# One sequence kernel's tables: the "into the states" table built from parameter rows in DRAM, and the scale moved to the "out of the states" table

## The chip, the cores and the metric

The kernel runs on one core of a Trainium2 chip. Its time is the device time of one execution in microseconds (us); the median of three runs before the change is 983.03 us (983.0 to 983.55). The core has a matrix engine (PE, whose weight loads are listed apart as PEld), a vector engine (DVE), an activation engine (ACT), a general engine (POOL) and SP, which here only issues DMA transfers. ACT and POOL issue transfers too. Each engine takes its instructions strictly in the order in which they were compiled, and an instruction whose input is late holds up all that stand behind it.

## The reference, cut to what matters

`x` is 64 batches by 64 heads by 1024 places. Each head is convolved causally with its own kernel of 1024 taps, a sum of 64 damped oscillations, after masking by a length per batch. What comes out goes through a mixture of 64 low-rank experts, 16 per token, and is added to `x`:

```python
dtA = A * dt[:, None]                       # A = -exp(log_A_real) + 1j * A_imag
P = dtA[:, :, None] * jnp.arange(length)
Cs = Cc * (jnp.exp(dtA) - 1.0) / A
K = 2.0 * jnp.einsum('hn,hnl->hl', Cs, jnp.exp(P)).real
...
y = irfft(rfft(u_m, n) * rfft(K, n))[..., :Lq] + u_m * D[:, None]   # then masked again
...
scores = xf @ Wr.T                          # xf = y, token by token
gates = softmax(top_k(scores, 16))
h = einsum('nd,krd->nkr', xf, A);  out = 2 * einsum('nkr,kdr->nd', h * G, B)
```

Everything is in float32.

## The kernel before, in words

The 64 heads are worked in 8 groups of 8; a group is 4 pairs of heads, and a pair fills 128 partitions (2 heads x 64 oscillations). The 1024 places are 8 blocks of 128. A convolution (`conv(g, ...)`) takes each pair through three parts. `into_states` multiplies the blocks of `x` by the table `bt` (products `pu`, place on the partitions) and ACT copies the result from PSUM to `s`; `recur` carries the states from block to block on DVE with the three columns `turn`; `inside` multiplies `x` with the Toeplitz matrix `toep` of a head's first 128 taps, and `across` adds to the same PSUM tile (`pc`) what comes out of the states by the table `w`. DVE masks the result into `y`.

`tables(g)` makes these tables. With the oscillation on the partitions and the place 0 to 128 along the free dimension it forms exp(place x dt_re) on ACT (`mag`), the turns place x tu (`f`, in two parts tu_hi and tu_lo), rounds and clamps them on DVE, and takes sine and cosine on ACT. The products of magnitude and circle are `w`. ACT and DVE then scale `w` by the pair's coefficients (`alpha`, `nbeta`, `nalpha`) into `b`; PE transposes `b` (tile `pb`, line 326), so that the place stands on the partitions, and ACT copies it to `bt` (lines 328 and 330). From `b` PE also sums the taps over the oscillations (`pk`, line 293); ACT copies them to `ks`, DVE adds D, and SP writes them to DRAM (`krows`, line 303) and reads them back as the Toeplitz matrix (line 305). In the first group all this is cut finer, since nothing else is there to run.

After a group's convolution, `gates(g, y)` finds its 16 experts per token (products `psh`, transposes `psc`, then a chain of DVE instructions), `spread_gates` spreads the gates over partitions through DRAM (`gx`, loads from POOL's queue), and `first(g, y, ...)` makes the first expert product: 14 products of 16 matmul records each (`h`, line 553), in four PSUM banks (`ps_f`). DVE and POOL add and gate these and POOL stores them. When all 8 groups are done, `second` makes the other expert product from what was stored.

**The order of the work.** The functions are generators: `conv` yields at places where the main loop issues one or more products of the group before, and it calls `step(n)` to issue n pieces of `tables(g + 2)`, the tables of the group after. This gives each instruction its rank. A planner then puts the instructions of each engine in order by simulated time: the first in rank of those that are ready. So ready work of a low rank can come early, where an engine would idle. Some instructions are pinned: `issue_after(i)` puts what a block holds for the engine of `i` behind `i`, on that engine alone; `keep_in_program_order` pins one instruction behind the one before it.

**Buffers.** `bt`, `toep`, `mag`, `f`, `k`, `sn` and `ks` have one buffer each; `w` and `turn` have two. The PSUM pool `ps_k` has two banks, shared by `pu`, `pb`, `pk`, `psh`, `psc` and `pg`. The loads of `x` (four buffers of a pair each) are issued by SP, and wait until `inside` of the pair that had the buffer is done.

Of the kernel before, what the change touches and what calls it, by code (L numbers as in the profile page):

```python
# [37 lines left out]
F32 = mybir.dt.float32  # L38
I32 = mybir.dt.int32
AF = mybir.ActivationFunctionType  # L40
# [4 lines left out]
P = 128  # L45
# [9 lines left out]
HG = 8  # L55
# [37 lines left out]
def body(ctx: ExitStack, tc, x, xo, lens, par, dvec, at, bm, wt, cst, out):  # L93
# [140 lines left out]
    tabs = {}  # L234
    scales = {}

    def tables(g):

        j0 = g * GP
        wide = [P, GP, NW]

        def new(t, name=None):
            return tabp.tile(wide, F32, tag=t, name=f"{name or t}_{g}")

        mag, f, k = new("mag"), new("f"), new("k")
        for i in range(GP):
            nc.scalar.activation(mag[:, i, :], lv, AF.Exp, scale=dt_re[:, j0 + i : j0 + i + 1])
        tt(f, tu_hi[:, j0 : j0 + GP].unsqueeze(2).to_broadcast(wide),  # L250
           lv.unsqueeze(1).to_broadcast(wide), ALU.mult)
        yield
        ts(k, f, MAGIC, ALU.add, MAGIC, ALU.subtract)
        yield
        tt(f, f, k, ALU.subtract)
        yield
        for i in range(GP):
            stt(f[:, i, :], lv, tu_lo[:, j0 + i : j0 + i + 1], ALU.mult, f[:, i, :], ALU.add)
            if i % 2:
                yield  # L260
        ts(f, f, HALF_IN, ALU.min, -HALF_IN, ALU.max)

        sh, sn = new("k", "sh"), new("sn")
        nc.scalar.activation(sh, f, AF.Sin, scale=math.pi)
        nc.scalar.activation(sn, f, AF.Sin, scale=2.0 * math.pi)
        nc.scalar.activation(sh, sh, AF.Square)
        nc.scalar.activation(sh, sh, AF.Copy, scale=-2.0, bias=1.0)
        yield
        w = tab2.tile([P, 2, GP, NW], F32, tag="w", name=f"w_{g}")
        tt(w[:, 1], mag, sn, ALU.mult)  # L270
        yield
        tt(w[:, 0], mag, sh, ALU.mult)
        yield
        alpha, nbeta, nalpha = (scales[q] for q in ("alpha", "nbeta", "nalpha"))
        bt = tp.tile([P, GP, 2 * P], F32, tag="bt", name=f"bt_{g}")

        def others():
            return (tab2.tile([P, 3, GP], F32, tag="turn", name=f"turn_{g}"),
                    tp.tile([P, HG, P], F32, tag="toep", name=f"toep_{g}"))

        if g == 0:
            turn, toep = others()
            tabs[g] = (w, bt, turn, toep)
        h0 = g * HG
        all_rows = tabp.tile([2, GP, P], F32, tag="ks", name=f"ks_{g}")

        def kernels(bbs, i):


            n = i + 2 * len(bbs)  # L290
            pk = ps_k.tile([2, n - i, P], F32, tag="pk", name=f"pk_{g}_{i}")
            for m, bb in enumerate(bbs):
                nc.tensor.matmul(pk[:, 2 * m : 2 * m + 2, :], lhsT=heads, rhs=bb[:, :, 0, :],  # L293
                                 start=True, stop=True)
            ks = all_rows[:, i:n, :]
            nc.scalar.copy(ks, pk)
            return ks, i, n

        def rows(ks, i, n):

            tt(ks[:, :, 0], ks[:, :, 0], d_sb[:, j0 + i : j0 + n], ALU.add)
            row = krows[h0 + 2 * i : h0 + 2 * i + 1, :]
            nc.sync.dma_start(
                krows[h0 + 2 * i : h0 + 2 * n, P - 1 :].rearrange("(i a) l -> a i l", a=2), ks)
            nc.sync.dma_start(toep[:, 2 * i : 2 * n, :],
                              bass.AP(row.tensor, row.offset, [[1, P], [KROW, 2 * (n - i)], [1, P]]))

        bbs, halves = [], []
        for i in range(GP):
            j = j0 + i  # L310
            re, im = w[:, 0, i, :P], w[:, 1, i, :P]
            if i % 2 == 0:
                bb = tabp.tile([P, 2, 2, P], F32, tag=("sn", "k")[i // 2], name=f"b_{g}_{i}")
                bbs.append(bb)
            b = bb[:, i % 2]
            for c, by in enumerate((alpha, nbeta)):
                if g == 0:
                    ts(b[:, c, :], re, by[:, j : j + 1], ALU.mult)
                else:
                    nc.scalar.activation(b[:, c, :], re, AF.Copy, scale=by[:, j : j + 1])  # L320
            stt(b[:, 0, :], im, nbeta[:, j : j + 1], ALU.mult, b[:, 0, :], ALU.add)
            stt(b[:, 1, :], im, nalpha[:, j : j + 1], ALU.mult, b[:, 1, :], ALU.add)
            if g == 0 or i % 2 == 0:
                pb = ps_k.tile([P, 1 if g == 0 else 2, 2 * P], F32, tag="pk", name=f"pb_{g}_{i}")
            for c in range(2):
                nc.tensor.transpose(pb[:, i % 2 if g else 0, (1 - c) * P : (2 - c) * P], b[:, c, :], ident)  # L326
            if g == 0:
                nc.scalar.copy(bt[:, i, :], pb[:, 0])
            elif i % 2:
                nc.scalar.copy(bt[:, i - 1 : i + 1, :], pb)  # L330
            if g == 0 and i % 2:
                halves.append(kernels(bbs[i // 2 :], i - 1))
            if g == 0 and i == 3:
                rows(*halves[0])
            yield
        if g:
            turn, toep = others()
        V.tensor_copy(turn[:, 0:2], w[:, :, :, P])
        ts(turn[:, 2], turn[:, 1], -1.0, ALU.mult)
        if g == 0:  # L340
            yield
            rows(*halves[1])
            return
        ks = kernels(bbs, 0)
        yield
        rows(*ks)
        tabs[g] = (w, bt, turn, toep)


    def new(name, w=NP, dtype=F32, keep=False):  # L350
# [117 lines left out]
    wa, wb = [], []  # L468
    marks = {}
    sums = factors_by_identity(*wa_quarters, wa)  # L470
    steps0 = tables(0)
    next(steps0)
    for _ in some(sums, 1):
        pass
# [3 lines left out]
    e_re = new("ere")  # L478
    n_re, n_im, t2 = new("nre"), new("nim"), new("t2")
    alpha, nbeta, nalpha = (new(n, keep=True) for n in ("alpha", "nbeta", "nalpha"))  # L480
    beta = new("beta")

    def products():
        ts(e_re, s2, -1.0, ALU.mult, 1.0, ALU.add)
# [27 lines left out]
        ts(nalpha, alpha, -1.0, ALU.mult)  # L512

    together(products(), some(steps0, 2))
    scales.update(alpha=alpha, nbeta=nbeta, nalpha=nalpha)

    for _ in some(sums, 7):
        pass
# [5 lines left out]

    def masks():
        lens_f = prep.tile([P, NB], F32, tag="lensf", name="lens_f")
        V.tensor_copy(lens_f, lens_sb)
        tt(mask, feat.unsqueeze(2).to_broadcast([P, NBLK, NB]),
           lens_f.unsqueeze(1).to_broadcast([P, NBLK, NB]), ALU.is_lt)
# [13 lines left out]
    def seven(fac, rf, j, name, finish, second_early=False):  # L543

        def product(n, bank=None, more=False):
            first = bank is None
            if first:
                bank = ps_f.tile([P, 2, HT], F32, tag="pf", name=f"{name}_{j}_{n}")  # L550
            for ii in range(2):
                for k in range(KH):
                    nc.tensor.matmul(  # L553
                        bank[:, ii, :],
                        lhsT=fac[n - 1][:, k, (j + ii) * P : (j + ii + 1) * P],
                        rhs=rf[n - 1][:, k, :],
                        start=(first and ii == 0 and k == 0),
                        stop=(ii == 1 and k == KH - 1 and not more),
                        skip_group_check=True,
                    )  # L560
            return bank

        def new(t, n=0):
            return fp.tile([P, 2, HT], F32, tag=t, name=f"{name}_{j}_{t}{n}")

        c11 = product(1, more=True)
        p1 = new("p", 1)
        nc.scalar.copy(p1, c11)
        yield
        if second_early:  # L570
            product(2, c11)
            yield
        p6 = product(6)
        u2 = new("u2")
        tt(u2, p1, p6, ALU.subtract)
        yield
        if not second_early:
            product(2, c11)
            yield
        p7 = product(7)  # L580
        u3 = new("u3")
        tt(u3, p7, u2, ALU.add)
        yield
        c12 = product(5, more=True)
        c22 = new("p", 5)
        stt(c22, u3, -1.0, ALU.mult, c12, ALU.subtract)
        yield
        p4 = product(4)
        yield
        product(3, c12)  # L590
        finish(j, c11, u2, u3, c12, p4, c22)
        yield


    def conv(g, steps, out):
# [89 lines left out]
        if g == 0:  # L685
            into_states(2)
            into_states(3)
            first_two = inside(0), inside(1)
            across(*first_two[0], True)
            across(*first_two[1])  # L690
            recur(2, 3)
            last_two = inside(2), inside(3)
            yield
            across(*last_two[0], True)
            across(*last_two[1])
            return
        yield
        step(4)
# [5 lines left out]
        recur(2, 3)  # L704
        out_of(1)
        yield
        step(5)
        yield
        out_of(2)
        yield  # L710
# [553 lines left out]
```

## Time and profile before

The profiled execution took 983.15 us; its span, from the first to the last instruction, is 981.3 us. The granted PE clock is full throughout.

| what | us |
|---|---|
| PE busy | 967.1 |
| DVE busy | 717.5 |
| ACT busy | 159.7 |
| POOL busy | 332.3 |
| start of the first `psh` of groups 0 to 7 | 51.0, 123.6, 185.3, 262.0, 338.7, 415.3, 492.0, 567.8 |

The time from one `psh` to the next is what one group takes: 76.7 us in groups 3 to 6. After 568 us only expert products follow, and the change doesn't reach them. Matmuls are pipelined: each record includes some waiting inside the engine, so the records of PE overlap, and the chain (which takes the time from one piece to the next) tells what an instruction adds. "Idle before" is an engine's idle time ahead of an instruction, with the one that ended it.

### The profile page before, as it was taken

To read this page: it belongs to the slowest core of one execution; us is meant where nothing else is said; L and a number is where in the kernel's file an instruction comes from. 1 tells how busy PE (TensorE), PEld (TensorE's weight loads), DVE (VectorE), ACT (ScalarE), POOL (GpSimd) and SP (SyncE) were. 2 spreads that over 40 slices of the span, in tenths; PEclk is the share of its full clock that TensorE was granted. 3 is DMA by queue.
4 is the path that set the end of the run, shared out by engine and by line. 5 is a ranking of instruction groups with operands and counts; after the bars stand their busy time and mean duration, and the time that the engine had idled before them with its cause. 6 is when DMAs were issued, how large, how long until landed. Compare 5 with 4: busy or idle time off the path is not lost.

```text
span 981.3 us, 11964 instructions
## 1 busy us (share of the span) xinstructions
PE 967.1 (99%) x4312; PEld 722.8 (74%) x4312; DVE 717.5 (73%) x1681; ACT 159.7 (16%) x310; POOL 332.3 (34%) x285
## 2 busy tenths in 40 slices
PE   7999999999999999999999999999999999999998
PEld 2476656676676686586676678888888888888887
DVE  8889698587487597587566669788866785686674
ACT  5245051420231231131001000000000000000000
POOL 0212121032023022122123112246645663754565
PEclk9999999999999999999999999999999999999999
DMA  7915243325315315415405254573674466268432
GB/s 279 235 50 162 73 150 105 108 81 161 108 70 145 126 41 156 140 55 156 135 27 166 76 177 161 200 290 110 214 258 130 169 207 232 88 215 269 128 117 98
DMA packets 67457, 143.99 MB, mean 147 GB/s; under 512 B 9479, under 2 KB 18247, under 8 KB 67399
## 3 DMA queue, kind: packets, MB, share of 16 engines
q1 hardware_dynamic: 49378, 94.40, 28.8%
q0 software_dynamic: 16864, 47.22, 15.5%
q10 hardware_dynamic: 1156, 1.61, 0.6%
q8 instruction: 34, 0.56, 0.2%
q14 instruction: 25, 0.20, 0.1%
HBM read 94.89 MB, written 47.25 MB: 145 GB/s over the span
## 4 chain that ended last, share of the span: by engine, by line
PE 94%; DVE 4%; DMA 0%; issue 0%; POOL 0%; ACT 0%; DVEq 0%
PE h L553 39%; PE s L1033 34%; PE pc L644 6%; PE pu L618 5%; PE pc L653 5%; PE psh L721 3%; PE pb L326 1%; PE pk L293 1%; DVE hg L355 1%; PE pg L765 0%; PE psc L730 0%; DMA par_sb<-in_par 0%; DVE y L661 0%; DVE ty L355 0%; DVE f L366 0%
## 5 line engine op out<-in xcount | busy, mean ns | idle before, releaser
L366 DVE SCALAR_TENSOR_TENSOR s<-s,turn 128x128 f32<-128x128 f32 (+1 forms) x558 | 142.9, 303 | 34.0 <-ACT s L623 28.0
L553 PE MATMUL h<-y,waa 128*128 128x256 f32 x512 | 121.8, 384 | 0.0
L553 PE MATMUL h<-ty,was 128*128 128x256 f32 x512 | 116.9, 381 | 0.0
L553 PE MATMUL h<-y,was 128*128 128x256 f32 x512 | 116.6, 381 | 0.0
L553 PEld LDWEIGHTS h<-y,waa 128*128 128x128 f32 x512 | 93.9, 190 | 28.7 <-issue 16.8
L553 PEld LDWEIGHTS h<-ty,was 128*128 128x128 f32 x512 | 96.5, 190 | 18.1 <-issue 5.4
L553 PEld LDWEIGHTS h<-y,was 128*128 128x128 f32 x512 | 96.5, 190 | 17.9 <-issue 5.2
L803 POOL TENSOR_TENSOR hg<-h_p,gx 128x512 f32<-128x512 f32 x16 | 27.0, 1689 | 218.6 <-DVE h_p L366 215.0
L803 POOL TENSOR_TENSOR hg<-h_u,gx 128x512 f32<-128x512 f32 x32 | 47.1, 1474 | 123.0 <-DVE h_u L355 122.2
L661 DVE TENSOR_TENSOR y<-pc,mask 128x512 f32<-128x512 f32 x64 | 42.3, 684 | 35.4 <-PE pc L653 35.4
L1047 ACT COPY p<-s 128x512 f32<-128x512 f32 x28 | 16.4, 586 | 312.9 <-PE s L1033 301.5
L900 POOL TENSOR_TENSOR o<-o,acc_a 128x512 f32<-128x512 f32 x32 | 48.0, 1519 | 42.7 <-DMA r<-hg_dram 10.8
L644 PE MATMUL pc<-x,toep 128*128 128x512 f32 x128 | 61.5, 605 | 0.0
L553 PE MATMUL h<-ty,waa 128*128 128x256 f32 x256 | 58.7, 381 | 0.0
L355 DVE TENSOR_TENSOR hg<-hg 128x512 f32<-128x512 f32 x64 | 42.8, 689 | 19.0 <-POOL hg L803 18.0
L776 POOL DMA_DIRECT2D gx<-gt_dram x56 | 33.5, 630 | 66.2 <-DMA gt_dram<-gt 66.2
L553 PEld LDWEIGHTS h<-ty,waa 128*128 128x128 f32 x256 | 47.9, 190 | 10.2 <-issue 3.9
L618 PE MATMUL pu<-x,bt 128*64 128x448 f32 x256 | 55.1, 553 | 0.0
L653 PE MATMUL pc<-s,w 64*128 64x448 f32 x248 | 54.7, 561 | 0.0
L355 DVE TENSOR_TENSOR o<-o,s 128x512 f32<-128x512 f32 (+1 forms) x53 | 35.6, 672 | 25.3 <-PE s L1033 18.8
L900 POOL TENSOR_TENSOR o<-o,b_room 128x512 f32<-128x512 f32 x32 | 49.9, 1581 | 9.8 <-DVE b_room L355 9.8
L623 ACT COPY s<-pu 128x448 f32<-128x448 f32 x62 | 33.0, 532 | 119.7 <-PE pu L618 119.6
(231 smaller groups left out, 1586.5 us busy)
## 6 DMA issues: line engine op xcount, KB each, us to landing
x<-in_x SPq DMA_DIRECT2D x32, 512.0 KB
hg_dram<-hg POOLq DMA_DIRECT2D x16, 1024.0 KB, 5.5
o<-in_xo SPq DMA_DIRECT2D x64, 256.0 KB
out<-o SPq DMA_DIRECT2D x63, 256.0 KB
gx<-gt_dram POOLq DMA_DIRECT2D x56, 256.0 KB, 6.3
qy<-hg_dram SPq DMA_DIRECT2D x28, 512.0 KB
r<-hg_dram SPq DMA_DIRECT2D x26, 512.0 KB
hg_dram<-hg POOLq DMA_DIRECT2D x16, 768.0 KB, 4.3
```

The source lines that it names most:

```text
L355: V.tensor_tensor(out=o, in0=a, in1=b, op=o_)
L366: V.scalar_tensor_tensor(out=o, in0=a, scalar=s, in1=b, op0=o1, op1=o2)
L553: nc.tensor.matmul(bank[:, ii, :], lhsT=fac[n - 1][:, k, (j + ii) * P : (j + ii + 1) * P], rhs=rf[n - 1][:, k, :], start=(first and ii == ...
L618: nc.tensor.matmul(pu[hh * NS : (hh + 1) * NS, :], lhsT=bt[:, i, (1 - c) * P + hh * NS : (1 - c) * P + (hh + 1) * NS], rhs=xt[:, hh, : NCH ...
L623: marks["s"] = nc.scalar.copy(s[:, c], pu.rearrange("p (k b) -> p k b", b=NB))
L644: nc.tensor.matmul(pc, lhsT=toep[:, 2 * i + hh, :], rhs=xt[:, hh, :], start=True, stop=False)
L653: m = nc.tensor.matmul(pcs[hh][:, NB:], lhsT=w[o : o + NS, c, i, 1:], rhs=s[o : o + NS, c].rearrange("p k b -> p (k b)"), start=False, sto ...
L661: marks["y"] = V.tensor_tensor(out=y[:, :, i // 2, 2 * (i % 2) + hh, :], in0=pcs[hh].rearrange("p (k b) -> p k b", b=NB), in1=mask, op=ALU ...
L776: i = queue.dma_start(gx[:, ii, :], gt_dram[g, c * n : (c + 1) * n, :].unsqueeze(1).to_broadcast([n, RANK, TOK]),)
L803: G.tensor_tensor(out=o, in0=a, in1=b, op=op)
L900: tc.keep_in_program_order(G.tensor_tensor(out=o, in0=a, in1=b, op=op_))
L1033: nc.tensor.matmul(bank[:, ii, :], lhsT=left_[i - 1][:, k, ii * P : (ii + 1) * P], rhs=right_[i - 1][:, k, :], start=(first and ii == 0 an ...
```

## The change

For the first group nothing changes but the names of buffers; `masks`, which runs on DVE during its convolution, also turns the sign of `nbeta` back into `beta`, which the later groups need. From the second group on, the table into the states is no longer scaled, transposed and copied. It is formed a second time, with the place already on the partitions, and without the coefficients; these go into the table out of the states instead (`o`, which takes the place of `w`), and the taps of the kernel are summed from `o`.

To form it, the parameters `dt_re`, `tu_hi` and `tu_lo` are needed as rows. Once, at the end of group 0's convolution, `parameter_rows` transposes the three on PE into one `ps_k` tile, copies it on ACT and writes it to DRAM (`trows`). Each group then loads its part of each row, repeated over all partitions, into the buffers of `mag`, `f` and the new one-buffer tile `turned`, and goes through exponential, rounding and circle again, with the scalar `place` (the partition's number) as factor. Two DVE products make `bt`. The pieces that `tables` yields are fewer (11 instead of 13), and the step in the middle of `conv` issues 6 instead of 5.

```diff
+    def circle(sh, sn, f, sign=1.0):
+        nc.scalar.activation(sh, f, AF.Sin, scale=math.pi)
+        nc.scalar.activation(sn, f, AF.Sin, scale=sign * 2.0 * math.pi)
+        nc.scalar.activation(sh, sh, AF.Square)
+        nc.scalar.activation(sh, sh, AF.Copy, scale=-2.0, bias=1.0)
...
+    def kernels(g, ks, re, i, n):
+        pk = ps_k.tile([2, n - i, P], F32, tag="pk", name=f"pk_{g}_{i}")
+        for m in range(0, n - i, 2):
+            nc.tensor.matmul(pk[:, m : m + 2, :], lhsT=heads, rhs=re[:, i + m : i + m + 2, :],
+                             start=True, stop=True)
+        nc.scalar.copy(ks[:, i:n, :], pk)
+
+    def rows(g, ks, i, n):
+        j, h = g * GP + i, g * HG + 2 * i
+        tt(ks[:, i:n, 0], ks[:, i:n, 0], d_sb[:, j : j + n - i], ALU.add)
+        nc.sync.dma_start(
+            krows[h : h + 2 * (n - i), P - 1 :].rearrange("(i a) l -> a i l", a=2), ks[:, i:n, :])
+
+    def toeplitz(g, toep, i, n):
+        row = krows[g * HG + 2 * i : g * HG + 2 * i + 1, :]
+        nc.sync.dma_start(toep[:, 2 * i : 2 * n, :],
+                          bass.AP(row.tensor, row.offset, [[1, P], [KROW, 2 * (n - i)], [1, P]]))
+
+    def tables(g):
...
+        mag, f, both_ = new("mag"), new("f"), turned(g)
+        k, sn = both_[:, 0], both_[:, 1]
+        for i in range(GP):
+            nc.scalar.activation(mag[:, i, :], lv, AF.Exp, scale=dt_re[:, j0 + i : j0 + i + 1])
...
+        ts(f, f, HALF_IN, ALU.min, -HALF_IN, ALU.max)
+        circle(k, sn, f)
+        yield
+        tt(sn, mag, sn, ALU.mult)
+        tt(k, mag, k, ALU.mult)
+        turn, toep = others(g)
+        V.tensor_copy(turn[:, 0:2], both_[:, :, :, P])
+        ts(turn[:, 2], turn[:, 1], -1.0, ALU.mult)
+
+        def row(t, n):
+            nc.sync.dma_start(flat(t), trows[n, j0 : j0 + GP, :].rearrange("j q -> (j q)").partition_broadcast(P))
+
+        mag, f = new("mag", "rmag"), new("f", "rf")
+        row(mag, 0)
+        row(f, 1)
+        yield
+        alpha, beta, nbeta = (scales[q] for q in ("alpha", "beta", "nbeta"))
+        o = tab2.tile([P, 2, GP, NW], F32, tag="w", name=f"w_{g}")
+        for i in range(GP):
+            j = j0 + i
+            for c, by in enumerate((alpha, beta)):
+                nc.scalar.activation(o[:, c, i, :], k[:, i, :], AF.Copy, scale=by[:, j : j + 1])
+            for c, by in enumerate((nbeta, alpha)):
+                stt(o[:, c, i, :], sn[:, i, :], by[:, j : j + 1], ALU.mult, o[:, c, i, :], ALU.add)
+            if i == 1:
+                yield
+        ks = rows_tile(g)
+        kernels(g, ks, o[:, 0, :, :P], 0, GP)
+        yield
+        both_ = turned(f"{g}r")
+        lo, place = both_[:, 1], feat[:, 0:1]
+        row(lo, 2)
+        mag, f, lo, k = flat(mag), flat(f), flat(lo), flat(both_[:, 0])
+        nc.scalar.activation(mag, mag, AF.Exp, scale=place)
+        ts(f, f, place, ALU.mult)
+        rows(g, ks, 0, GP)
+        yield
+        ts(k, f, MAGIC, ALU.add, MAGIC, ALU.subtract)
+        tt(f, f, k, ALU.subtract)
+        yield
+        stt(f, lo, place, ALU.mult, f, ALU.add)
+        ts(f, f, HALF_IN, ALU.min, -HALF_IN, ALU.max)
+        circle(k, lo, f, -1.0)
+        yield
+        bt = tp.tile([P, GP, 2 * P], F32, tag="bt", name=f"bt_{g}")
+        for c, t in enumerate((lo, k)):
+            tt(bt[:, :, c * P : (c + 1) * P], mag.rearrange("p (i q) -> p i q", q=P),
+               t.rearrange("p (i q) -> p i q", q=P), ALU.mult)
+        yield
+        toeplitz(g, toep, 0, GP)
+        tabs[g] = (o, bt, turn, toep)
...
     def masks():
         lens_f = prep.tile([P, NB], F32, tag="lensf", name="lens_f")
+        ts(beta, nbeta, -1.0, ALU.mult)
...
+    def parameter_rows():
+        pr = ps_k.tile([NP, 3, P], F32, tag="pk", name="par_rows")
+        for n, v in enumerate((dt_re, tu_hi, tu_lo)):
+            nc.tensor.transpose(pr[:, n, :], v, ident)
+        r = tabp.tile([NP, GP, P], F32, tag="ks", name="par_rows_sb")[:, :3, :]
+        nc.scalar.copy(r, pr)
+        nc.scalar.dma_start(trows.rearrange("k j q -> j k q"), r)
...
             across(*last_two[0], True)
             across(*last_two[1])
+            with tc.issue_after(marks["s"].ins):
+                parameter_rows()
             return
...
-        step(5)
+        step(6)
```

`marks["s"]` is, at that place, the last ACT copy of `s` in the first group's convolution.

## The prediction

> **What bounds the kernel now.** I read the busy shares first, then the chain that ended last.
>
> ```profile
> span 981.3 us, 11964 instructions
> PE 967.1 (99%) x4312; PEld 722.8 (74%) x4312; DVE 717.5 (73%) x1681; ACT 159.7 (16%) x310; POOL 332.3 (34%) x285
> ...
> PE 94%; DVE 4%; DMA 0%; issue 0%; POOL 0%; ACT 0%; DVEq 0%
> ```
>
> The matmul engine is the bound almost everywhere, so time is gained by taking work off PE, and lost where PE is made to wait. The chain in order of time prices what the change removes; this is its stretch around the end of one group's convolution:
>
> ```profile
> 322.37 0.22 PE pb L326 x2
> 322.59 3.46 PE h L553 x16
> ...
> 336.54 0.81 PE pb L326 x6
> 337.34 0.43 PE h L553 x2
> 337.78 0.96 PE pk L293 x4
> 338.73 3.58 PE psh L721 x16
> ```
>
> Eight transposes per group lie on the chain. Two take 0.22 us, so one holds PE for 0.11 us; six between a narrow product and h take 0.81, of which 0.15 is the turn from the 64-row form, which whatever comes next pays too.
>
> How much room the other engines have is read by stretches (the stretch and its length in us; then PE, PEld, DVE, ACT, POOL busy):
>
> ```profile
> 20.00:31.00 11.00, 10.41 (x47) 3.31 (x48) 10.65 (x48) 6.94 (x16) 3.20 (x3) 1.00 0.55 123
> 75.00:108.00 33.00, 33.00 (x145) 20.87 (x146) 32.54 (x104) 13.60 (x28) 5.52 (x5) 1.00 0.39 126
> 108.00:122.00 14.00, 14.00 (x60) 8.49 (x59) 6.61 (x12) 0.81 (x2) 4.52 (x4) 1.00 0.24 70
> 122.00:137.00 15.00, 12.58 (x61) 8.22 (x60) 14.62 (x48) 4.73 (x8) 0.77 (x1) 1.00 0.45 163
> ...
> 262.00:339.00 77.00, 77.00 (x343) 52.59 (x344) 54.78 (x158) 17.39 (x35) 17.40 (x18) 1.00 0.35 112
> ```
>
> In a settled group (last line) PE is full and DVE has 22 us free. Only early on, at 75 to 108 and at 122 to 137, is DVE full, and in the latter PE loses 2.4 us.
>
> **PE, part by part.** Removed: 7 groups x 8 transposes x 0.11 = 6.2 us. The two `pk` products per group stay, with the same columns. Added once: three transposes of the parameter table, 3 x 0.11 = 0.3. Net -5.9.
>
> Here the Trainium skill differs: "TensorE: Matmul & The Clock Gate", Part 4 (PE-mode transpose), gives a 128x128 transpose about 275 ns in a kernel's context. The row agrees as a record's length, 283 ns mean (groups by line and shape over the first 540 us, busy us, mean ns, then idle before; the others price what follows):
>
> ```profile
> L326 PE MATMUL pb<-cst_sb,b 128*128 128x128 f32 x64 | 11.0, 283 | 0.9 <-DVE b L366 0.6 <-ACT s L623 0.3
> ...
> L264 ACT ACT_TABLE_LOAD x7 | 9.0, 1283 | 1.2 <-DVE f L362 1.1
> ...
> L366 DVE SCALAR_TENSOR_TENSOR h_p<-h_u,h 128x512 f32<-128x512 f32 x13 | 8.9, 683 | 11.7 <-PE h L553 11.7
> ...
> L355 DVE TENSOR_TENSOR f<-f,k 128x516 f32<-128x516 f32 x8 | 5.5, 692 | 0.1
> ...
> L264 ACT ACTIVATE sh<-f 128x516 f32<-128x516 f32 x8 | 5.1, 633 | 5.4 <-DVE f L362 5.4
> ...
> L362 DVE TENSOR_SCALAR k<-f 128x516 f32<-128x516 f32 x8 | 3.4, 425 | 3.7 <-PE pk L293 3.7
> ```
>
> By the page's price 56 would be worth 15.4 us (about 968 us); but records overlap, and start to start they are 110 ns apart. I take the 6.2.
>
> **DVE.** From the second group on, the eight scalings b become eight of o, one column wider, and the two products w are done in place: no change. Added per group, 512 wide: three TENSOR_SCALAR (times place, round, clamp) at 0.425, two TENSOR_TENSOR at 0.69 for bt and one for f-k, one SCALAR_TENSOR_TENSOR at 0.683: 1.28 + 2.07 + 0.68 = 4.0 us, 28 over seven groups. In a settled group 54.8 becomes 58.8 of some 76: the idle DVE time hides it, and without that cover it would be 4 us a group. The sign flip of beta is one small instruction (0.18 us by its neighbours) on the full DVE of the first group; I count 0.1.
>
> **ACT.** Added per group: one exponential and four of `circle`, 5 x 0.63; removed: two bt copies at 0.59. Net 2.0, 14 over seven; with two more table switches a group, 14 x 1.283 = 18. ACT goes from 160 to about 192 of 980: hidden, except where a copy of `s` or `p` queues behind a switch (1.3 us). PE has products of 3.46 us to run meanwhile, so 0 to 0.3 us a group; I take 0.
>
> **DMA and queues.** Three loads of 256 KB a group on SP, 21 in all, 5.4 MB beside 144: bandwidth is no matter. SP's time goes mostly into waiting for pc to free x buffers (372.7 us in all); the loads stand in the same queue as x, the kernel-row write and the Toeplitz load. x is issued about 31 us ahead of its use (the issues begin at 308 and the last at 335; `pu` of the next group would follow at 367), so a few us of queueing there cost nothing. POOL's queue is not touched. The row write comes earlier, before the last rounding; the Toeplitz load stays behind the last `inside`, as now. `bt` no longer waits for PE and ACT: two DVE products after the fourth `into_states`, some 50 us ahead of use.
>
> What the trace doesn't show is how late these loads land. Nearest is a load of the same size, 2 KB rows repeated over partitions:
>
> ```profile
> gx<-gt_dram POOLq DMA_DIRECT2D x56, 256.0 KB, 6.3
> ```
>
> The skill's page "DMA: Bandwidth & Descriptors" (Anatomy of one DMA) fits about 2.0 us fixed plus bytes over 436 GB/s for loads from POOL's queue: an estimate of 2.6 for one alone. If the instruction order was planned on 2.6 and the chip takes 6.3, then the ACT exponential, the DVE `f * place` and the step with `lo` stand 3.7 us at the head of their queues, per load. `f * place` would be due where DVE idles. The `lo` step falls among the gates' top-16 work: behind it h_u and h_p wait, then PE's four `pf` banks, which cover about one product (3.46). Bounds: 0 by the page; 2 x 3.7 - 3.46 = 4 us a group, 28 in all, if nothing else hides it. I take 0.1 us a group, 0.7 in all: the eight gx loads are issued together and slow each other, these are not.
>
> **The first group.** `parameter_rows` puts its three transposes into a tile of `ps_k`, which has two banks. Its last input, tu_lo, is done at 9.3 us, and PE then still waits for weights now and again, so the planner, which fills idle engines with what is ready, can place them there; but the ACT copy that frees the bank is queued behind the last `s` copy. Until then every transpose, `pk` and `pu` of group 0 shares the other bank. The rows now:
>
> ```profile
> 22.89 0.53 ACT L623 COPY s<-pu 128x448 f32<-128x448 f32 x1 [0.56 <-PE pu L618]
> 23.64 0.53 ACT L623 COPY s<-pu 128x448 f32<-128x448 f32 x1 [0.22 <-PE pu L618]
> ```
>
> With two banks the copies follow each other by 0.75 to 0.86; with one, a `pu` takes 1.02 on PE (21.87 to 22.89), 0.53 for the copy and 0.05 to begin again: 1.6. Over 8 `pu`, 4 `pb` and 2 `pk` the last copy moves from 30.6 to about 39 us. DVE's recurrences, which run unbroken from 24.2 to 42.8, absorb part: the first pair would end at 35, the second at 46, 3 us later. PE fills with the first h product, so I put the loss at 2.5 us; bounds 0 (placed after the copies) and 5 (nothing absorbed). What is late next is the last y and with it the first gates, 51.0 to about 53.5.
>
> Group 1's tables are made against time, at 48 to 75. The new chain (o, loads, second rounding, second circle) ends about where `bt` does now, 71 to 76; `pu` starts at 74.9, with h products left to fill. I count 0, and 2 if they run out.
>
> **Sum.** -5.9 - 0 + 2.5 + 0.7 + 0.1 = -2.6 on the profiled span, 981.3 to 978.7. That execution took 983.15, close to the median of 983.03, so I carry the difference over: 980.4.
>
> **Rivals.**
> 1. The transposes of the parameters are placed late, and the bank is never held. Then -5.1: 977.9. For it: nothing forces them early. Against: other ready products are seen running ahead of their turn, such as the two h at 337.34 before `pk`.
> 2. *Slower:* late row loads. The wait at `lo` (and at the exponential) reaches PE each group. It decides the sign as soon as it costs more than 3.3 / 7 = 0.47 us a group; at 1.2 us, time is 983.0 - 3.3 + 8.4 = 988. For it: 6.3 against 2.6, and queues that can't overtake. Against: 22 us of DVE idle per group.
> 3. The gain doesn't arrive: around 122 to 137 the chain runs through DVE and not PE, so transposes removed ahead of it buy only a longer wait, and 8 us more DVE work falls between 48 and 137. With the bank cost at its upper end: 983.0 - 5.9 + 5 + 1 = 983.
>
> **Chances.** Forecast 0.36, first rival 0.16, second 0.28, third 0.20. A measurement of this kernel can tell about 0.2% (2 us): faster means below 981.1. The forecast and the first rival give nearly all of 0.5; the third and some of the forecast 0.2 same; the second and the rest of the third 0.3 slower. The range takes in the first rival's floor (the turns into and out of transposes gained too, 976.5) and the second at 1.2 us a group: 976.5 to 988; the forecast alone would be 979 to 982.
>
> **What would show it.** Right: no `pb` on PE after group 0, and a settled group 0.9 us shorter between two `psh`. DVE near 746 us, ACT near 192. The parameter transposes in front of the first `pu`, `s` copies about 1.6 us apart, the first `psh` near 53.5. Wrong: PE or DVE idle behind a DMA of the rows (second rival); first `psh` still at 51 (first); stretch 122 to 137 longer by more than 2 us (third). A settled group with PE idle at all would break the sum, since every cover I named lies there.

## The result, and the profile after

The changed kernel takes 990.26 us (median of 6 runs, 988.92 to 990.86), the kernel before 983.13 in the same comparison: a ratio of 1.0070, 95% interval 1.0057 to 1.0083. It is slower by 0.7%, where I forecast 0.3% faster; 990.3 lies above the range of 976.5 to 988. The profiled execution took 989.06, its span is 987.3. From the page of the kernel after, the span, the busy line and the shares of the chain:

```profile
span 987.3 us, 11992 instructions
...
PE 966.7 (98%) x4259; PEld 717.3 (73%) x4259; DVE 739.1 (75%) x1731; ACT 191.2 (19%) x346; POOL 333.5 (34%) x285
...
PE 87%; DVE 9%; DMA 2%; ACT 1%; issue 1%; POOL 0%; DVEq 0%; ACTq 0%
```

ACT's sum came out as forecast (191); DVE rose by 21.6 us and not by 28, in part because the records that I added up overlap (one of 0.69 us is followed after 0.61). PE's share of the chain fell from 94% to 87%; 9% now runs through DVE and 2% through transfers. PE is no less busy than before, though 56 transposes are gone.

Where it happens is read from the starts of the eight `psh`, which close each group's convolution. Before: 51.0, 123.6, 185.3, 262.0, 338.7, ... After: 51.3, 125.7, 192.3, 268.8, 345.2, ... A settled group is 0.25 us shorter (76.4 for 76.7). The stretch from the first to the third `psh`, in which the second and third group are convolved, is 6.7 us longer. The windows of that place after the change (stretch and length; PE, PEld, DVE, ACT, POOL busy; granted clock):

```profile
115.00:120.00 5.00, 2.98 (x11) 1.47 (x9) 3.79 (x8) 2.56 (x5) 1.26 (x1) 1.00 0.00 0
120.00:125.00 5.00, 3.06 (x13) 1.37 (x12) 3.39 (x8) 1.34 (x3) 0.48 (x1) 1.00 0.46 105
125.00:130.00 5.00, 4.32 (x10) 1.23 (x12) 1.97 (x4) 3.67 (x9) 0.79 (x1) 0.50 0.65 213
130.00:135.00 5.00, 5.00 (x23) 2.87 (x20) 5.00 (x9) 1.27 (x4) 0.00 (x0) 0.82 0.00 0
```

PE idles 4 of 10 us, and then 5 us are spent at clock 0.50 and part of the next 5 too. The 16 records of `psh` take 6.67 us here instead of 3.65. Over the stretch between the first and the third `psh` PE idles 7.1 us (2.4 before): +4.7, and +3.0 from the half clock; 24 transposes fewer (three groups) give 2.6 back, and 1.6 more is PE work that fell into this stretch. Of this, 0.4 is two more matmuls of h, and some 0.9 would be the new place of `pk` at 0.3 a group (`rfe_pk` below). This is the profiled execution alone: in two of the six the granted clock averaged 0.999 (0.995 or 0.996 in the others), and they took 988.92 and 990.86, no less than the rest. So the loss does not need the half clock, and what stood in its place there no trace shows.

What PE waits for is `y`, DVE's multiplication of the convolution's banks with the mask: it frees the two `pc` banks and is what `psh` reads. And `y` stands behind table work in DVE's queue. The chain in order of time, after the change:

```profile
115.16 2.05 DVE f L436 x4
...
117.74 1.28 ACT L306
...
119.03 0.63 ACT turned L306
119.67 0.52 ACT turned L307
...
121.41 0.71 DVE turned L425
...
122.13 4.12 DMA rmag<-trows
...
126.32 1.28 ACT L400
```

These are the fourth group's tables, made while the second group's last banks wait. DVE does `f`, waits for ACT's table switch and circle, and multiplies; SP issues the row loads meanwhile. The first of the two last `y` pairs starts at 117.6 behind `f`, though its banks were complete at 112.6, the last one at 124.4 behind the product of `rf` with the place, though its banks were complete at 122.0. The waits on DVE and on ACT between 112 and 130 (us in total, times, longest):

```profile
DVE w L436 <- ACT w L388: 3.0, 1, 3.0
DVE turned L425 <- ACT turned L307: 1.4, 1, 1.4
DVE rf L430 <- DMA rf<-trows: 0.8, 1, 0.8
...
ACT L400 <- DMA rmag<-trows: 4.9, 1, 4.9
```

In a settled group the same chain is harmless, but another thing shows, at its end:

```profile
340.39 1.72 PE pc L726 x4
342.10 1.75 PE pc L735 x8
343.86 1.28 DVE y L743 x2
345.14 0.04 issue
345.18 1.07 PE psh L805 x3
```

PE has nothing to do during the last `y` and idles 0.3 us. Before, six transposes, two h and `pk` stood exactly there.

### The profile page after: what moved, and what is told of

The parts are those of the page before. It is cut to its first block, busy times and chain, and to the rows that moved or that the text cites. A ratio compares the mean times of both kernels' runs of the same rounds, so it can differ in the third digit from the quotient of the medians.

```text
span 987.3 us, 11992 instructions
## 1 busy us (share of the span) xinstructions
PE 966.7 (98%) x4259; PEld 717.3 (73%) x4259; DVE 739.1 (75%) x1731; ACT 191.2 (19%) x346; POOL 333.5 (34%) x285
## 4 chain that ended last, share of the span: by engine, by line
PE 87%; DVE 9%; DMA 2%; ACT 1%; issue 1%; POOL 0%; DVEq 0%; ACTq 0%
PE h L624 35%; PE s L1117 34%; PE pc L726 5%; PE pc L735 5%; PE pu L700 5%; PE psh L805 3%; DVE s L436 2%; DVE y L743 1%; DMA rmag<-trows 1%; DVE hg L425 1%; PE pk L323 1%; DMA gx<-gt_dram 1%; DVE f L436 1%; DVE ty L425 0%; DVE w L436 0%
## 5 line engine op out<-in xcount | busy, mean ns | idle before, releaser
L436 DVE SCALAR_TENSOR_TENSOR s<-s,turn 128x128 f32<-128x128 f32 (+1 forms) x558 | 145.4, 307 | 23.4 <-ACT s L705 18.8
L984 POOL TENSOR_TENSOR o<-o,acc_a 128x512 f32<-128x512 f32 x32 | 48.1, 1521 | 42.6 <-ACT acc_a L1002 21.6
L425 DVE TENSOR_TENSOR hg<-hg 128x512 f32<-128x512 f32 x64 | 43.0, 686 | 22.4 <-POOL hg L887 21.6
```

Of the source, the lines that this page charges most:

```text
L425: V.tensor_tensor(out=o, in0=a, in1=b, op=o_)
L436: V.scalar_tensor_tensor(out=o, in0=a, scalar=s, in1=b, op0=o1, op1=o2)
L984: tc.keep_in_program_order(G.tensor_tensor(out=o, in0=a, in1=b, op=op_))
```

## Experiments

Every variant was planned anew, so its order can differ in places that the edit does not name. The theories: **A**, table work stands ahead of `y` in DVE's order, PE idles, and the idling halves the clock. **B**, the row loads land late. **C**, 28 us more DVE work is too much. **D**, part of the transposes' worth lay in the shadow of `psh`'s wait for `y`. All times are medians; before is 983.0 to 983.4 in each comparison.

**The fourth group's tables held behind `y`** (`gate3`). The convolution of a group makes the tables of the next: `g == 2` is the third group's, and its first four steps are the fourth group's tables.

```
+        if g == 2:
+            with tc.issue_after(marks["y"].ins):
+                step(4)
+        else:
+            step(4)
```

> The changed kernel, complete; only the first four table steps of the fourth group (made during the third group's convolution) are held on DVE behind the last y of the second group's convolution. Theory A (most of the loss is DVE's order there: new table work stands ahead of the y that psh waits for, PE idles, and then runs at half clock for some us): third psh at about 186 instead of 192.3, granted clock 1.00 in 125 to 135, total 990.3 - 6 = 984. Theory B (late row loads): the loads keep their latency and only move, total 989 to 991. Theory C (28 us more DVE work is simply too much): 989 to 991. Settled groups by all three: 76.4 as in the changed kernel.

Measured: 989.86 (ratio 1.0045 to 1.0102). The second `psh` came at 120.6 instead of 125.7, so the order was what held it. But the next window took 72.3 instead of 66.7. Its chain, at the third group's `y`:

```profile
179.87 5.52 DMA rf<-trows
...
185.41 0.48 DVE rf L430
185.89 0.61 DVE y L743
186.50 0.04 issue
186.55 2.07 PE pc L726 x2
```

Now the fifth group's `rf` stood at the head of DVE, 5.5 us after its issue. PE idled 3.5 and then 2.6 us, and the clock was at half from early in the second. A is right about the place, and B about what makes it long; the loss moved on by a group.

**No row loads** (`noloads`).

```
-        mag, f = new("mag", "rmag"), new("f", "rf")
-        row(mag, 0)
-        row(f, 1)
...
-        row(lo, 2)
...
-        nc.scalar.activation(mag, mag, AF.Exp, scale=place)
+        nc.scalar.activation(mag, mag, AF.Exp, scale=dt_re[:, j0 : j0 + 1])
```

> The changed kernel without its 21 row loads: the exponential and the second rounding take what stands in the same buffers (other values, same instructions, no wait for a transfer). DVE still has the fourth group's table work ahead of the second group's last y. Theory A: only the waits for rows go (0.8 us on DVE ahead of y, about 3 us on ACT and DVE behind it); PE still idles ahead of the psh at 125.7 and the clock still drops: 987 to 988.5. Theory B: nearly the whole loss of 7 goes: 983 to 984.5. Theory C: 990.

Measured: 983.19 (ratio 0.9992 to 1.0009). So the loads, with the order that goes with them (some DVE steps changed places), carry 7.1 us: as much as the changed kernel is slower than the one before, as B said. A's 987 to 988.5 was wrong. The two idle stretches did not go away, they only became shorter:

```profile
115.00:120.00 5.00, 3.55 (x12) 1.36 (x12) 3.51 (x8) 4.06 (x6) 0.00 (x0) 1.00 0.04 8
120.00:125.00 5.00, 3.70 (x18) 1.59 (x18) 4.93 (x10) 3.88 (x10) 1.26 (x1) 1.00 0.61 205
125.00:130.00 5.00, 5.00 (x26) 3.63 (x23) 5.00 (x19) 0.59 (x1) 0.00 (x0) 1.00 0.00 0
```

PE still idles 2.75 us of 10, but the clock stays at 1.00. In the changed kernel, the instructions ahead of the last `y` waited 1.9 us for ACT's circle and only 0.8 for rf; the waits add up in one queue. Settled groups are 76.4 with and without loads, so there the waits for rows cost nothing.

**Less added DVE work** (`lessdve`): the product with the place, the rounding and its subtraction and the step with `lo` are deleted.

> The changed kernel without four of the seven added DVE instructions of a group: the product with the place, the rounding and its subtraction, and the step with lo (0.43 + 0.43 + 0.69 + 0.68 = 2.2 of 4.0 us a group); loads stay, nothing waits for lo's any more. Theory C: a good half of the loss goes, 986 to 987. Theory A: the table work that stands ahead of y at 112 to 122 is the first circle's and stays, 988 to 989.5. Theory B: the waits at lo go (2 us in a settled group), the exponential's stay: 988 to 989, and if the settled groups lose by lo, they come to 76.1 or less.

Measured: 987.43 (ratio 1.0023 to 1.0049). The number alone would suit C, the trace does not: PE idles 5.5 us in one piece at 115, for a `y` that stands behind 2.5 us of waits for ACT's circle and 1.5 for `rf`, whose load landed 3.8 us after its issue. The clock fell here too (0.77 in 115 to 120, 0.54 in 120 to 125), in part within the idle stretch itself, and the other stretch, ahead of `psh`, shrank to 0.3. Nothing in the settled groups changed (76.4).

**The transposes alone** (`before_nopb`), on the kernel before:

```
+            elif i % 2:
+                nc.scalar.copy(bt[:, i - 1 : i + 1, :], bb.rearrange("p i c q -> p i (c q)"))
```

in place of the transposes into `pb`.

> The kernel before with the transposes of the second to the eighth group left out alone: ACT copies b unturned into bt (other values, the same shapes), all else as it was. My sum: 56 x 0.11 = 6.2 less, 976.9, a settled group 75.8 instead of 76.7. The other theory (D: most of the eight stand in the shadow of psh's wait for the last y): a settled group gains 0.2 to 0.4, total 980.5 to 982.

Measured: 978.01 (ratio 0.9925 to 0.9958), 5.0 us less, between the two expectations. A settled group takes 76.1: 0.55 gained of the 0.9 that left PE, and PE now waits at `psh`:

```profile
PE psh L720 <- DVE y L660: 0.4, 1, 0.4
```

D is right in kind: two fifths of the worth in a settled group. In all it is a fifth, since the stretch from the first to the third `psh` gained 3.2 us, more than its 24 transposes (2.6); the order changed there too.

**The load of rf made early, first try** (`rfe`): rf goes into the buffer of the kernel rows.

```
+        rf = tabp.tile([P, GP, P], F32, tag="ks", name=f"rf_{g}")
+        row(rf, 1)
         mag, f, both_ = new("mag"), new("f"), turned(g)
```

with `ts(f, flat(rf), place, ALU.mult)` and `pk` behind it, and the exponential behind the second circle.

> The changed kernel, complete, with the waits for rows taken away without leaving anything out: the row rf is loaded into the buffer of the kernel rows, at the start of a group's tables and not behind its first circle; the exponential of rmag stands behind the second circle; pk follows the product with the place. Theory B' (late rows: the rf load, issued behind the first circle, lands 4 to 5.5 us later, stands at the head of DVE's queue ahead of the y that pc and psh wait for, and PE, idle for some 4 us, then runs at half clock): nearly all that leaving the loads out won, 983.5 to 984.5, clock 1.00 from 110 to 140. Theory A (table work ahead of y, loads or not, costs the most): 987 to 988.5, since the first circle's steps still stand there.

Measured: 1013.18 (ratio 1.0287 to 1.0317). It did not become early: in the settled groups SP issues it behind rmag's, which waits for the products with mag. The chain there, and windows around two such places in the same run:

```profile
268.50 0.62 DVE turned L426
...
269.58 6.78 DMA rf<-trows
...
276.78 0.69 DVE y L744
...
277.52 2.08 PE pc L727 x2
```

```profile
275.00:280.00 5.00, 2.48 (x4) 0.98 (x6) 1.68 (x3) 0.00 (x0) 0.00 (x0) 0.64 0.32 120
280.00:285.00 5.00, 4.85 (x16) 1.90 (x16) 2.08 (x6) 2.04 (x7) 0.00 (x0) 0.68 0.67 210
...
355.00:360.00 5.00, 3.82 (x15) 1.77 (x15) 1.68 (x3) 2.00 (x2) 0.00 (x0) 1.00 0.92 340
```

An accident that prices the mechanism. Where PE idled 3.3 us (at 274.2, and 3.4 at 434.6), the group took 82.5, 6.1 more than 76.4; where it idled 1.2 us (at 356.7), 77.9, which is 1.5 more. The extra idle time is 2.1; the other 2.5 us are left for the half clock.

**pk behind the second circle as well** (`rfe_pk`).

> As the one before, and in each group the products pk (and the write of their rows) moved behind the second circle, so that they can fill PE's wait for the last y. If part of the transposes' worth is lost in the settled groups because PE waits at psh for y while pk pays its own turn further up: a settled group 76.1 instead of 76.4 and 1.2 to 1.5 us in all, about 982.5. If the wait at psh is not what pk's place costs: 76.4 and 984.

Measured: 985.28 (ratio 1.0014 to 1.0027), not the 982.5. The settled group is 76.1, as expected from `pk`'s place, and DVE does not wait for rf anywhere between 110 and 190. But at 117 PE idles 4.3 us for a `y` behind the products with mag, which wait 2.0 us for ACT's circle: A without a wait for a load, followed by half clock (0.53 in 120 to 125).

```profile
PE pc L728 <- DVE y L745: 4.3, 1, 4.3
...
DVE turned L427 <- ACT turned L307: 2.0, 1, 2.0
```

**And the fourth group's tables held** (`rfe_pk_gate3`).

> As the one before, and the fourth group's first table steps held on DVE behind the second group's last y. Theory A as the smaller part (DVE's order at 112 to 122 costs PE 2.7 us of idle time even where no load is waited for): 2 to 3 us less, 979.5 to 980.5, below the kernel before. If holding them back only moves the loss to the third group's y, as it did where rows were late: 982.5 or more.

Measured: 983.47 (ratio 0.9994 to 1.0012). The window to the second `psh` shrank from 78.3 to 72.7, the next one grew from 59.3 to 63.9: waits on PE and DVE between 130 and 190:

```profile
PE pc L728 <- DVE y L745: 2.1, 1, 2.1
...
DVE turned L427 <- ACT turned L307: 3.3, 2, 2.0
```

The same pair of products, one group on. (0.66 of the clock was granted in the 5 us after this stretch.)

**PE kept busy ahead of psh** (`fill`): 20 useless transposes ahead of the second group's `psh`.

> The changed kernel, complete, with 20 useless transposes (20 x 0.11 = 2.2 us of PE work, nobody reads them) right ahead of the psh at 125.7, where PE idles 2.6 us. If the half clock after that idle time is what costs 3 us: the 16 psh records again 429 ns apart and not 847, granted clock 1.00 in 125 to 135, and the kernel is faster by the useless work, about 987. If the clock falls for another reason (the idle time at 116 alone, or none of it): clock 0.5 as before and 990 to 990.5.

Measured: 992.63 (ratio 1.0074 to 1.0135). The `psh` records, which start in pairs, did return to 423 ns from pair to pair, as the idle stretch ahead of them was filled. But in this run the clock fell after the first stretch already (2.07 us of idle time at 115.7; 0.79 in 115 to 120), and a later stretch of 3.6 us ahead of `pg`, at 140, brought it down once more. The plan also moved four matmuls of h from ahead of `psh` to behind it. That the half clock follows the idle time is supported, its price is not measured by this run.

**The loads left late, DVE's order changed** (`gate_rows`): holds for two groups' first steps, and

```
-        step(6)
+        step(3 if g in (1, 2) else 6)
...
         out_of(2)
...
         out_of(3)
+        if g in (1, 2):
+            with tc.issue_after(marks["y"].ins):
+                step(3)
```

> The changed kernel, complete, its row loads where they were (rf issued behind the first circle). Only DVE's order is changed, in three places: the fourth and the fifth group's first steps stay behind the last y of the convolution before, and the third and fourth group's steps from the product with the place on behind the last y of the convolution that they are made in. If the loss is table work (a load or a circle that it waits for) standing ahead of y on DVE, its latency as such is harmless: PE idles no more than about 2 us ahead of any pc or psh, the clock stays 1.00, and the total falls by 6 to 7, to 983.5 to 984.5. If the latency of the rows costs time wherever it stands (the tables come too late for the next group's pu, or ACT's wait for rmag holds up the copies of s): 987 to 990.

Measured: 986.03 (ratio 1.0008 to 1.0034). The third `psh` came at 184.4, 7.9 us earlier than in the changed kernel and 0.9 earlier than in the kernel before, with all loads in it. So latency behind `y` is harmless there. But the next window took 81.4: the held tables fell into the gates' stretch, where DVE was busy for 24.9 of the 29 us from 184 to 213, and ACT's copy of `gt`, which the next `pu` waits for, came last behind them:

```profile
213.32 0.62 DVE turned L425
213.96 2.45 ACT w L388 x8
216.41 0.48 ACT gt L858
216.93 1.19 PE pu L700 x4
```

**Three groups' tables held, rows early** (`rfe_pk_gate234`).

> The version with rf loaded early, the exponential behind the second circle, pk late, and the first steps of the fourth, fifth and sixth group's tables (instead of the fourth alone) held behind the last y of the convolution before. In the run with the fourth alone, PE idled 2.1 us at 179 for a y behind the fifth group's circle and then ran at half clock. If that is the rest of the loss: the third convolution's window 60 to 61 instead of 63.9, in all about 980 to 980.5, below the kernel before. If something else follows on: 982.5 to 983.5.

Measured: 990.7 (ratio 1.0051 to 1.0081). The third convolution's window is 59.8, as expected, and the two windows behind it 81.5 and 81.4, for the same reason as above. Holding whole tables is the wrong means.

**More DVE time ahead of psh** (`again2`, `again5`): one `y` of the last pair in each of three settled groups is done again two or five times.

```
-            for hh in range(2):
+            for hh in (0,) * (2 if i == GP - 1 and g in (3, 4, 5) else 0) + (0, 1):
```

> The changed kernel, complete, with one y multiplication of each of three settled groups (the fourth to the sixth) done three times instead of once, ahead of the last: 2 x 0.63 = 1.3 us of DVE time ahead of what psh waits for, where PE already waits 0.3. If PE's idle time costs only itself: 3 x 1.3 = 3.8 us more than the changed kernel, 994. If an idle stretch of 1.6 us already halves the clock: 3 us more for each, 1003.

> The same with five repeats: 5 x 0.63 = 3.2 us ahead of psh in three groups. If idle time costs only itself: 3 x 3.2 = 9.5 more than the changed kernel, 999.8. If an idle stretch of 3.4 us is followed by half clock for some 16 records of psh, as at 125.7 in the changed kernel: 3 us more for each, about 1009, and the psh records 850 ns apart instead of 429.

Measured: 990.08 and 989.71 (ratios 1.0039 to 1.0073, 1.0043 to 1.0085): nothing at all is lost against the changed kernel. The planned order answered the added work: six and twenty-two more h matmuls were put ahead of the first of these `psh` (230 and 246 in that window instead of 224). (The profiled execution of `again5` was its slowest, 995.1; 5.2 of that were lost ahead of the first `psh`.) So up to 9.5 us of DVE time on this very path are hidden, which speaks against C in the settled groups. That only time which the plan doesn't hold is left in the open is a reading; no run tests it.

**One row at a time** (`no_rf`, `no_rmag`): one load of the three is deleted.

> The changed kernel without the load of rf alone (the second rounding takes what stands in f: other values, same instructions); rmag and lo are loaded as before. If rf at the head of DVE ahead of y is what makes PE idle long enough for half clock: psh at about 124.5 instead of 125.7, no half clock, 985 to 986.5. If it is rmag (ACT's wait of 4.9 us, then DVE's for w): 989 to 990.

> The changed kernel without the load of rmag alone (the exponential takes what stands in mag); rf and lo are loaded as before. If rf is the cause: 988.5 to 990, half clock still at 125 to 131. If rmag is: 985 to 986.5, with the gap at 142 gone and no half clock.

Measured: 990.53 and 989.19 (ratios 1.0056 to 1.0081, 1.0044 to 1.0070). Neither alone wins back more than about 1 us, where all three loads together win 7 (that of lo was not tried alone; DVE waited 4.5 us for it in the second to fourth group's tables, but PE did not idle there by more than 0.9 us at a time). The waits between 112 and 130 say why. Without rf:

```profile
ACT L399 <- DMA rmag<-trows: 4.8, 1, 4.8
DVE w L435 <- ACT w L387: 4.2, 1, 4.2
...
PE psh L804 <- DVE y L742: 1.3, 1, 1.3
```

Without rmag:

```profile
PE psh L804 <- DVE y L742: 3.4, 1, 3.4
...
DVE rf L429 <- DMA rf<-trows: 1.6, 1, 1.6
```

Without rf, `psh` waits 1.3 us as in the run without loads; then ACT's wait for rmag delays the copy `sh` (PE idles 2.0 us at 129) and DVE's gates (2.7 us at 140, then half clock). Without rmag, `psh` waits 3.4 us and runs at half clock. Each late row was enough for one idle stretch that the clock answered.

**Both, with the order mended in one place** (`order_and_rows`): `rfe_pk_gate3`, and in the fourth group's convolution, which makes the fifth group's tables, the two products with mag are held behind the last `y` of the third group. Without the hold they ran early, ahead of that `y`.

```
         step(4)
...
+        if g in (3,):
+            with tc.issue_after(last_y):
+                step(1)
+            step(5)
```

(`last_y` is the last `y` of the convolution before.)

> The version with rf loaded early, the exponential behind the second circle, pk late and the fourth group's first steps held behind the second group's last y; new against that version: in the third convolution the two products with mag (they wait for ACT's first circle of the fifth group) are held behind the last y of the second group's convolution... that is, of the convolution before the one they are made in, and so go from ahead of the third group's y to behind it; nothing else on DVE moves. If table work that waits for ACT, ahead of y, is the whole of the rest: no gap at 179, clock 1.00 from 110 to 200, the window of that convolution 60 to 61 instead of 63.9, in all 980 to 981, below the kernel before. If the held products make the next tables late, as in the run that held whole tables: 983 or more.

Measured: 981.18 (22 runs; ratio 0.9982, 0.9972 to 0.9992), below the kernel before, with nothing left out. PE's order stayed as it was; on DVE only those two products and what hangs on them moved, from ahead of the last `y` pair to behind it (ACT's exponential of rmag and its copy of `ks` came later too), and 2.3 us went:

```profile
51.30:124.00 72.70, 70.55 (x305) 45.44 (x304) 64.95 (x189) 35.46 (x64) 15.73 (x18) 1.00 0.44 123
124.00:183.80 59.80, 58.96 (x252) 36.32 (x252) 53.55 (x164) 24.34 (x44) 10.28 (x13) 1.00 0.51 146
183.80:260.00 76.20, 75.75 (x334) 51.73 (x334) 58.05 (x169) 24.79 (x45) 17.63 (x18) 1.00 0.42 126
```

PE idles 2.2, 0.8 and 0.5 us, the clock is 1.00 throughout. This version is still 3.2 us above the kernel before without its transposes (978.01). ACT still waits some 29 us for rmag over the run; behind the second circle that holds up nothing that PE needs.

## Why the prediction was wrong

**The step that failed is "DMA and queues".** I saw that the loads might land 3.7 us later than planned, and priced it at "0.1 us a group, 0.7 in all", because `f * place` "would be due where DVE idles". It is worth 7.1 (`noloads`). Twice wrong: the place, and its shape. It isn't a small cost in every group; it is nothing in the settled ones, and two or three idle stretches in the second and third group, where the tables stand close ahead of the last `y`. I looked for the danger at `lo` and the gates; it was at `rf` ahead of `y`, and at rmag ahead of ACT's copies.

**The half clock was missing from the sum.** In the profiled execution it is 3.0 us, `psh` at half speed. No idle stretch before the change brought it on, and I gave a wait only its own length. Its share of the median loss stays open, since two executions were as slow without it.

**PE, -5.9:** measured -5.0 for the transposes alone. The term left out is the shadow: transposes filled the wait for the last `y`. The changed kernel keeps less still, 0.25 of 0.9 in a settled group, since `pk` moved up, pays its own turn there (0.3, `rfe_pk`), and no longer fills that wait.

**DVE, 28 us counted as nothing:** right in the settled groups (`again2`, `again5`). Not so between 51 and 192: averaged room says nothing of what stands ahead of what. Without any load PE still idled 3.3 us between the first two `psh`, where it had idled 0.6.

**What the loads do not explain.** Without them the kernel takes 983.2, but leaving the transposes out of the kernel before gave 978.0. These 5.2 us are a second part of the miss. In the traces they are 4.3: 1.2 in four settled groups (76.4 for 76.1, the place of `pk`) and, after 0.9 for four more matmuls of h, 3.2 between the first and the third `psh`, where PE idled 4.2 us and not 2.7. The rest of it was not taken apart.

**The first group, +2.5:** did not come. The parameter transposes ran at 47.4, behind the convolution, the `s` copies kept their distance, and the first `psh` moved by 0.2. The first rival was right in that alone.

**The rivals.** The second, late row loads, named the cause; its total (988) is nearest, and its point of decision, 3.3 us in all, was exceeded. But it put the wait at `lo` and the exponential, in every group; the exponential's did matter, but not in the settled groups. The third put the trouble near the right place (122 to 137; it was 115 to 132) and left out how long it would get.

## What to carry to other kernels

A wait that comes out longer than the order was planned for (here, it seems, for a transfer's landing or for ACT's circle) costs most at the head of a queue whose next entry frees the bound engine: look for what stands behind the waiting instruction, group by group, and first where the waiting engine is full. Moving two small products behind that entry was worth 2.3 us here; holding back the whole chain only carried the loss to the next group. And before work is taken off the bound engine, look whether it fills a wait that stays.

## What the runs showed of the hardware

After short idle times PE ran at half clock. Over these runs, no idle stretch of less than 2.0 us ahead of a matmul was followed by it; of eight between 2.0 and 2.2 us three were, one of 2.5 was not; of those of 2.6 us and more all were. The length alone does not decide. In all 17 traces the granted clock changes only at whole multiples of 3.41 us from its first entry, at 10.7 to 13.7 us. Three such windows of the changed kernel, and one of `again5` (clock: the number before the last two):

```profile
114.73:118.14 3.41, 1.57 (x8) 1.04 (x6) 3.34 (x7) 0.98 (x3) 1.53 (x1) 1.00 0.00 1
...
121.56:124.97 3.41, 1.50 (x8) 0.68 (x4) 2.51 (x7) 0.00 (x0) 0.45 (x1) 1.00 0.62 136
124.97:128.38 3.41, 2.69 (x8) 0.84 (x10) 0.66 (x2) 2.05 (x3) 0.81 (x1) 0.50 0.94 307
```

```profile
129.76:133.17 3.41, 1.85 (x10) 0.71 (x12) 1.50 (x3) 1.17 (x1) 1.26 (x1) 1.00 0.95 267
```

PE busy for 1.57 us of a window was still followed by full clock, 1.50 by half. Counted over all windows at full clock up to 8 us before the end, each of the 21 with PE busy for 44% or less was followed by half clock, and none of those with 46% or more. The half clock lasted one window, or two where PE had been busy for less than 88% of the first. So one stretch of 2.5 us that straddles two windows can go unpunished (`again5`), and one of 2.03 us that falls into one is not (`again2`). The Trainium skill ("TensorE: Matmul & The Clock Gate", Part 1) has the half rate come after an idle window of about 3.4 us; here the window did not have to be idle throughout. Two windows cost 3.0 us in the changed kernel and some 2.5 in `rfe`; one costs `psh` 1.7 in `no_rmag`.

The 256 KB row loads on SP that something waited for landed 3.0 to 4.0 us after their issue in the settled groups of the changed kernel, and up to 6.1 in its crowded part, 6.9 in `rfe` and 8.0 in `order_and_rows`. The estimate from the skill's "DMA: Bandwidth & Descriptors" (Anatomy of one DMA, a fit for POOL's queue) was 2.6, and the gx row's 6.3 is the median of eight loads issued together: in the kernel before, the first of eight took 3.8 us and the last 7.6. What remains open is which durations the plan itself assumed for them; no run shows that.
